# Three layer normalizations of layer 0 applied by ScalarE instead of VectorE

## The chip, the core and the metric

The kernel runs on one core of a Trainium2 chip, as a single launch. A core has five engines that run side by side, each with its own queue of instructions: TensorE (PE in the profile, with its weight loads as PEld), VectorE (DVE), ScalarE (ACT), GpSimd (POOL) and SyncE (SP), which here only issues DMAs. An engine takes its instructions in the order in which the program lists them; it waits at an instruction until the semaphores that this instruction names are reached. The metric is the time on the device in microseconds (us), lower is better.

## The reference, cut to what matters

Two layers over 4 sequences of 1024 tokens with 256 features, all fp32. Each layer computes `x = x + s * silu(...)` from a normalized `xn`:

```python
xn = _layernorm(x)                       # no gain, no bias
s = _L0_attn_ref(xn, ...)                # attention over cos/sin features, then an MLP
g = _silu(_L0_ffn_ref(xn, ...))          # token-shift FFN
x = x + s * g
xn = _layernorm(x)
s = _L1_attn_ref(xn, ...)                # selective scan (16 states, 512 channels)
g = _silu(_L1_ffn_ref(xn, ...))          # 8 experts, 2 per token, each with a norm
x = x + s * g
```

Inside `_L0_attn_ref` two more norms stand, both with gain and bias: `x2 = LN(x)` ahead of the queries, keys and values, and `x2 = LN(x + attention)` ahead of the MLP. Applying a norm to a token is `(x - mean) * rstd`, which is also `rstd * x + (-mean * rstd)`: a scale and a shift for each token.

## The kernel before

Layer 0 works on blocks of 512 tokens (`TB`), eight in all, two for each sequence. A block is a tile of 128 partitions with 4 x 256 numbers: a partition holds four tokens (`NT` = 4), and so a norm is applied with four instructions of 128x256, each with its own mean and rstd per partition. `normalize` (L499 to L518) gets them: bn_stats and bn_aggr on VectorE, the variance plus eps, then a power of -1/2 on GpSimd (L509). `apply` (L520) does `(x - mean) * rstd` on VectorE; all its instructions carry line L522.

There are four applies for each block:

- The attention norm (tile `x`, statistics `mv_a`, `rs2_a`), in `before_attention`. Two norms are folded into one here.
- The token norm (tile `x`, statistics `mv_a`, `rs_a`, kept from the attention norm), at the start of `after_attention`, on a block that is fetched anew. PE transposes its result (`tr_xnb`), and ACT copies that to `xnt`.
- The x3 norm (tile `x3_b` from `x`, statistics `mv_b`, `rs_b`), after the attention output is added. Right behind it VectorE adds a bias to the same `x` (L617). PE transposes x3 (`tr_b`), ACT writes `x3t`, and the MLP follows.
- The gate norm (tile `x`, statistics `mv_cb`, `rs_cb`), at the end of the block. Its result goes to HBM (`xn_d`), through PE (`tr_gb`) and ACT (`xg_b`) to the expert gate (`pgt_b`, added to `gate` at L715) and to the scan's input `xt_d`.

The attention itself runs in 64 groups of features (`cycle`): PE projects (`fk`, `fq`), ACT rounds (L764), VectorE takes the fraction (L765) and its magnitude (L397), ACT takes two sines, PE accumulates (`kv`, `pa`). The sines and the exponentials of the scan are in different tables of ACT, which is why there are 134 table loads (L488).

The scan of layer 1 runs beside layer 0 as soon as the first block is ready. A step of a unit (16 steps to a unit, 16 units) is: ACT takes two exponentials (the decays `da`, up to three steps ahead), VectorE multiplies (L1014), scans (L1017 or L1023) and multiplies again (L1032), and PE transposes and sums the result in PSUM (`y`). The steps between (L914 to L932) prepare a unit. When the last gate is there, VectorE computes the routes, GpSimd scatters the tokens to slots, and the experts' tiles run beside the rest of the scans (`es`, L1334, is the first thing that VectorE does with an expert's output). Their norm, too, is applied on ACT, with scale and shift (L1389 and L1391).

The order on each engine isn't that of the code. `arrange` (at the end of the kernel) takes all instructions with their dependences, plays them through with costs of its own, and writes an order for PE, VectorE and ACT by hand as scheduling dependences. Among the instructions that are ready on an engine, the one with the lowest due time goes first; the due time is the place in the code plus an entry of the table `LATER`, by engine and by the name of the tile written (for ACT in layer 0: `x` 47, `xi` 189, `da` 415). What it assumes for an instruction's cost:

```python
if engine == "Activation":
    w = 165 + 0.84 * n + 75 * min(scalars, 1)
...
    w = 160 + (1.053 if psum else 0.516) * n + 60 * scalars      # tensor_scalar on DVE
```

The small statistics and shifts come from the pool `small`, two buffers to a tag.

Of the kernel before, what the change touches and what calls it, by code (L numbers as in the profile page):

```python
# [15 lines left out]
F32 = mybir.dt.float32  # L16
U32 = mybir.dt.uint32
AF = mybir.ActivationFunctionType
ALU = mybir.AluOpType
# [4 lines left out]
P = 128  # L24
# [3 lines left out]
NT = TB // P  # L28
# [336 lines left out]
def kernel(  # L365
# [3 lines left out]
    nc = tc.nc  # L369
# [19 lines left out]
    def col(name, i=0):  # L389
        return vec[:, COL[name] + i : COL[name] + i + 1]  # L390

    def tokens(ap):
        return ap.rearrange("(t p) d -> p t d", p=P)
# [15 lines left out]
    small = ctx.enter_context(tc.tile_pool(name="small", bufs=2))  # L409
# [13 lines left out]
    def fetch_x(j):  # L423
        t = work.tile([P, NT, D], F32, name=f"x_{j}_{nc.next_id()}", tag="w")
        nc.gpsimd.dma_start(out=t, in_=tokens(x[j * TB : (j + 1) * TB, :]))
        return t
# [71 lines left out]
    def normalize(pool, src, tag, twice=False):  # L498


        st = small.tile([P, NT, 6], F32, name=f"st_{tag}", tag="ln_st")
        bufs = 4 if twice else 2
        mv = pool.tile([P, NT, 2], F32, name=f"mv_{tag}", tag="ln_mv", bufs=bufs)
        rs = pool.tile([P, NT], F32, name=f"rs_{tag}", tag="ln_rs", bufs=bufs)
        for t in range(NT):
            nc.vector.bn_stats(st[:, t, :], src[:, t, :])  # L506
            nc.vector.bn_aggr(mv[:, t, :], st[:, t, :])
        nc.vector.tensor_scalar(rs, mv[:, :, 1], EPS, None, ALU.add)
        nc.gpsimd.tensor_tensor(rs, rs, mhalf, ALU.pow)  # L509
        if not twice:  # L510
            return mv, rs
        both = small.tile([P, NT], F32, name=f"rs2_{tag}", tag="ln_rs2")
        nc.vector.tensor_tensor(both, rs, rs, ALU.mult)
        nc.vector.tensor_tensor(both, both, mv[:, :, 1], ALU.mult)
        nc.vector.tensor_scalar(both, both, EPS, None, ALU.add)
        nc.gpsimd.tensor_tensor(both, both, mhalf, ALU.pow)
        nc.vector.tensor_tensor(both, both, rs, ALU.mult)
        return mv, rs, both  # L518

    def apply(dst, src, mv, rs):  # L520
        for t in range(NT):
            nc.vector.tensor_scalar(  # L522
                dst[:, t, :], src[:, t, :], mv[:, t, 0:1], rs[:, t : t + 1], ALU.subtract, ALU.mult
            )
# [9 lines left out]
    keys, kept = {}, {}  # L534

    def bias(n, tiles=NT):

        return bias_s[:, n : n + 1, :].to_broadcast([P, tiles, D])

    def before_attention(b, s):  # L540
# [5 lines left out]
        mv, rs, both = normalize(keep, xi, tag, twice=True)  # L546
        kept[j] = (mv, rs)
        apply(xi, xi, mv, both)
        yield "N"
        x2t = work.tile([P, NC, TB], F32, name=f"x2t_{tag}", tag="w")  # L550
# [31 lines left out]
    def after_attention(b, s, at):  # L582

        j = b * (L // TB) + s
        tag = f"b{j}"
        x1 = fetch_x(j)
        yield "N"
        apply(x1, x1, *kept.pop(j))
        yield "N"
        xnt = keep.tile([P, NC, TB + 1], F32, name=f"xnt_{tag}", tag="xnt")  # L590
        if s == 0:
# [21 lines left out]
        yield "N"  # L613
        mv, rs = normalize(small, x1, tag)
        x3 = work.tile([P, NT, D], F32, name=f"x3_{tag}", tag="w")
        apply(x3, x1, mv, rs)
        nc.vector.tensor_tensor(x1, x1, bias(2), ALU.add)  # L617
        yield "N"
        x3t = work.tile([P, NC, TB], F32, name=f"x3t_{tag}", tag="w")
        for c in range(NC):  # L620
            nc.scalar.activation(
                x3t[:, c, :], transposed(x3, c, f"{tag}{c}"), AF.Identity,
                bias=col("ln2_b", c), scale=col("ln2_g", c),
# [72 lines left out]
        xi = fetch_x(j)  # L696
# [2 lines left out]
        nc.vector.tensor_tensor(x1, x1, xi, ALU.add)  # L699
        nc.gpsimd.dma_start(out=tokens(x_mid[j]), in_=x1)  # L700
        mv, rs = normalize(small, x1, f"c{tag}")
        apply(xi, x1, mv, rs)
        nc.gpsimd.dma_start(out=tokens(xn_d[j]), in_=xi)
        yield "N"
        xt = work.tile([P, NC, TB], F32, name=f"xg_{tag}", tag="w")
# [824 lines left out]
    for b in range(NB):  # L1530
        groups = [("k", b, s, t) for s in range(2) for t in range(NT)]
        groups += [("q", b, s, m, par) for s in range(2) for m in range(NC) for par in range(2)]
        for c, group in enumerate(groups):
            if c == 0:
                before.add(before_attention(b, 1))
            elif c == 4:
                while before.force():
                    pass
            elif c == 12 and b + 1 < NB:
                before.add(before_attention(b + 1, 0))  # L1540
            if before.wants == "K" and c >= 12:
                before.wants = "N"
            cycle(group, quota=(2, 3 if scans.ahead else 6, 2 if scans.ahead else 6, 0))
            for s in range(2):
                if len(at.get((b, s), ())) == NC:
                    after.add(after_attention(b, s, at.pop((b, s))))
            if 0 in ready and not blocks and not scans.side.todo:
                scans.side.add(first_unit())
                while not units:
                    scans.side.force()  # L1550
        while before.force():
            pass
# [87 lines left out]
```

## Time and profile before

| | us |
|---|---|
| median of 3 runs | 2220.71 |
| lowest and highest | 2216.21, 2221.44 |
| the profiled execution, its own run | 2219.3 |
| its span, first to last instruction | 2217.6 |
| PE busy | 1776.2 (80%) |
| DVE busy | 1939.0 (87%) |
| ACT busy | 1389.7 (63%) |
| POOL busy | 501.2 (23%) |
| mean granted TensorE clock | 0.88 |

The profile is of one execution. A slice line gives an engine's busy share in 40 equal slices of the span, in tenths. A group's row reads: line, engine, operation, out<-in, shapes and count; then after the first bar the busy time of all of them together and the mean length of one in ns (neighbours overlap a little, so busy time divided by the count is less than the mean); after the second bar the time that the engine stood idle just before them, and what ended it. In the timeline each row is the start, the length and the instruction, and in square brackets the idle time before it with what released it. A row of the window view gives the length, then busy us and instruction counts of PE, PEld, DVE, ACT and POOL, then the granted clock, the share of the DMA engines, and GB/s.

### The profile page before, as it was taken

The page shows a single profiled execution, that of the slowest core. Times are in us where ns is not written, and L with a number is a line of the kernel's source. Part 1 is how long each engine was busy: PE and PEld are TensorE (multiplying, and loading weights), DVE is VectorE, ACT ScalarE, POOL GpSimd, SP SyncE. Part 2 cuts the span into 40 slices and gives each one's busy share as a digit, 9 for nine tenths or more (in the row PEclk, how much of TensorE's full clock was granted, in tenths as well). Part 3 has the DMA queues.
Part 4 walks back from the last instruction along what each step waited for, and adds up shares of the span by engine and source line. Part 5 has one row for each costly group of instructions (what it writes and reads, how often), then busy time and mean ns, then how long its engine had stood idle before and what let it go on. Part 6 is the DMA issues. An engine that isn't in the chain of part 4 may idle for free. (4 is left out here: it accounts for less than half of the span.)

```text
span 2217.6 us, 25392 instructions
## 1 busy us (share of the span) xinstructions
PE 1776.2 (80%) x9192; PEld 1232.7 (56%) x9192; DVE 1939.0 (87%) x2508; ACT 1389.7 (63%) x2039; POOL 501.2 (23%) x459
## 2 busy tenths in 40 slices
PE   6789679789987889969888777367988879899754
PEld 3335346444654545645456555256777658778643
DVE  4582669999999899889999999858998999989998
ACT  4664468797887788697875264334554555455584
POOL 1000100101100111000010110844544435445210
PEclk9789789789998989979998796588999989999877
DMA  9601123323332332323334354666777857877553
GB/s 274 170 19 48 57 87 103 107 68 95 83 108 85 115 86 78 105 75 107 114 89 136 117 159 128 164 200 202 227 243 222 240 200 247 280 230 224 190 191 103
DMA packets 145086, 320.22 MB, mean 144 GB/s; under 512 B 23344, under 2 KB 43952, under 8 KB 139072
## 3 DMA queue, kind: packets, MB, share of 16 engines
q1 hardware_dynamic: 110704, 170.02, 28.8%
q0 software_dynamic: 34256, 148.58, 19.3%
q8 instruction: 73, 1.20, 0.2%
q14 instruction: 53, 0.43, 0.1%
HBM read 256.86 MB, written 61.69 MB: 144 GB/s over the span
## 5 line engine op out<-in xcount | busy, mean ns | idle before, releaser
L496 ACT ACTIVATE da<-dt,neg_a 128x512 f32<-128x512 f32 x512 | 336.0, 715 | 157.1 <-PE y L1035 101.1
L1035 PE MATMUL y<-ident,da 128*128 128x128 f32 x2048 | 304.6, 298 | 126.8 <-DVE da L1032 120.3
L1035 PEld LDWEIGHTS y<-ident,da 128*128 128x128 f32 x2048 | 257.8, 154 | 193.3 <-DVE da L1032 95.8
L1032 DVE TENSOR_TENSOR da<-h,bcs 128x1024 f32<-128x1024 f32 x256 | 311.2, 1217 | 0.9
L1017 DVE TENSOR_TENSOR_SCAN h<-da,h 128x1024 f32<-128x1024 f32 x128 | 290.9, 2281 | 10.7 <-ACT da L496 8.8
L1014 DVE TENSOR_TENSOR h<-dtu,bcs 128x1024 f32<-128x1024 f32 x240 | 287.8, 1212 | 9.9 <-DMA bcs<-bcd 9.3
L1023 DVE TENSOR_TENSOR_SCAN h<-da,h_tail,h 128x512 f32<-128x512 f32 x224 | 277.2, 1268 | 8.8 <-ACT da L496 8.0
L403 PE MATMUL ph<-xst,we 128*128 128x256 f32 x736 | 178.9, 396 | 10.0 <-ACT xst L1309 9.3
L488 ACT ACT_TABLE_LOAD x134 | 171.9, 1283 | 3.2 <-PEq L1625 0.8
L403 PE MATMUL po<-we,ht 128*128 128x256 f32 x736 | 171.0, 385 | 1.1 <-ACT ht L1321 0.9
L403 PEld LDWEIGHTS ph<-xst,we 128*128 128x128 f32 x736 | 141.7, 198 | 34.6 <-ACT xst L1309 12.9
L403 PEld LDWEIGHTS po<-we,ht 128*128 128x128 f32 x736 | 139.6, 193 | 31.0 <-issue 6.6
L403 PE MATMUL ph_b<-x3t_b,w_b 128*128 128x512 f32 x256 | 119.8, 618 | 9.6 <-DVE fs_k L765 5.2
L403 PE MATMUL py_b<-w_b,ht_b 128*128 128x256 f32 x512 | 116.8, 385 | 4.7 <-ACT ht_b L643 1.7
L1321 ACT ACTIVATE ht<-ph,we 128x256 f32<-128x256 f32 x184 | 76.7, 470 | 65.0 <-PE ph L403 52.2
L403 PEld LDWEIGHTS py_b<-w_b,ht_b 128*128 128x128 f32 x512 | 97.4, 193 | 23.2 <-ACT ht_b L643 3.4
L801 PE MATMUL kv<-fs_k,v_a 128*32 128x256 f32 x1024 | 84.2, 475 | 29.6 <-ACT fs_k L496 29.6
L1309 ACT COPY xst<-pxs 128x512 f32<-128x512 f32 x46 | 26.9, 585 | 120.6 <-PE pxs L1305 120.6
L1272 POOL DMA_INDIRECT fused<-xs x46 | 86.4, 1878 | 44.5 <-DVE xs L1338 32.0
L1272 POOL DMA_INDIRECT slots<-xs x46 | 89.8, 1953 | 18.5 <-issue 10.1
L765 DVE SCALAR_TENSOR_TENSOR fs_k<-fs_k,fk 128x512 f32<-128x512 f32 x128 | 80.0, 678 | 15.7 <-ACT fs_k L764 15.7
L832 PE MATMUL pa<-fs_q,kvp 128*32 128x512 f32 x512 | 83.5, 675 | 12.5 <-ACT fs_q L496 12.5
(239 smaller groups left out, 3388.9 us busy)
## 6 DMA issues: line engine op xcount, KB each, us to landing
bcs<-bcd SPq DMA_DIRECT2D x240, 512.0 KB, 5.2
xs<-slots POOLq DMA_DIRECT2D x23, 516.0 KB, 4.9
x<-in_x_dram POOLq DMA_DIRECT2D x23, 512.0 KB, 5.2
slots<-blank SPq DMA_DIRECT2D x1, 11776.0 KB, 48.9
w_b<-in_w_dram POOLq DMA_DIRECT2D x16, 512.0 KB, 4.4
w_b<-in_w_dram POOLq DMA_DIRECT2D x32, 256.0 KB, 3.0
xs<-slots POOLq DMA_DIRECT2D x23, 260.0 KB, 3.9
slots<-blank SPq DMA_DIRECT2D x1, 5888.0 KB, 26.2
```

The source lines that it names most:

```text
L403: nc.tensor.matmul(ps, lhs, rhs, start=i == 0, stop=i == len(pairs) - 1)
L488: nc.scalar.preload_act_table_set({"E": "natural_log_exp_and_others", "S": "silu_and_others"}[which])
L496: in_turn(nc.scalar.activation(out, in_, func, **kw))
L765: nc.vector.scalar_tensor_tensor(t[:, 1, :], t[:, 0, :], -ROUND, ps[r], ALU.add, ALU.subtract)
L801: nc.tensor.matmul(kv[b][r // 2][32 * g : 32 * g + 32, r % 2, :, :], v[:, t, h * DH : (h + 2) * DH], f[:, :, m, par, :], start=(s, t, r % ...
L832: nc.tensor.matmul(pa[b, s][32 * r : 32 * r + 32, :], kvp[b][:, e, 4 * m + r, par, :], features(fs, r)[:, e, :], start=(par, e) == (0, 0), ...
L1014: nc.vector.tensor_tensor(h, dtu, bcs[:, 0:1, :].to_broadcast([P, UNIT, TB]), ALU.mult)
L1017: nc.vector.tensor_tensor_scan(flat, da.rearrange("p w t -> p (w t)"), flat, 0.0, ALU.mult, ALU.add)
L1023: nc.vector.tensor_tensor_scan(h[:, w, :], da[:, w, :], b[w], h_tail[:, c, n : n + 1], ALU.mult, ALU.add,)
L1032: nc.vector.tensor_tensor(da, h, bcs[:, 1:2, :].to_broadcast([P, UNIT, TB]), ALU.mult)
L1035: nc.tensor.matmul(y[:, t, w * P : (w + 1) * P], da[:, w, t * P : (t + 1) * P], ident, is_transpose=True, start=False, stop=(n, t % 2, w) ...
L1272: i = nc.gpsimd.indirect_dma_start(out=dst, out_offset=IndirectOffsetOnAxis(ap=index, axis=0), in_=src, in_offset=None)
```

## The change

A new helper, `apply_by_scalar`, computes the shift `-mean * rstd` for the four tokens of each partition with one small instruction on VectorE (128x4), and then applies scale and shift with four activations (Identity) on ScalarE. The token norm, the x3 norm and the gate norm use it; the attention norm stays on VectorE.

```diff
+    def apply_by_scalar(dst, src, mv, rs, tag):
+        shift = small.tile([P, NT], F32, name=f"shift_{tag}", tag="ln_shift")
+        nc.vector.scalar_tensor_tensor(shift, mv[:, :, 0], -1.0, rs, ALU.mult, ALU.mult)
+        for t in range(NT):
+            nc.scalar.activation(
+                dst[:, t, :], src[:, t, :], AF.Identity, bias=shift[:, t : t + 1],
+                scale=rs[:, t : t + 1],
+            )
+
     def apply(dst, src, mv, rs):
         for t in range(NT):
             nc.vector.tensor_scalar(
...
         x1 = fetch_x(j)
         yield "N"
-        apply(x1, x1, *kept.pop(j))
+        apply_by_scalar(x1, x1, *kept.pop(j), f"k{tag}")
...
         x3 = work.tile([P, NT, D], F32, name=f"x3_{tag}", tag="w")
-        apply(x3, x1, mv, rs)
+        apply_by_scalar(x3, x1, mv, rs, f"b{tag}")
         nc.vector.tensor_tensor(x1, x1, bias(2), ALU.add)
...
         mv, rs = normalize(small, x1, f"c{tag}")
-        apply(xi, x1, mv, rs)
+        apply_by_scalar(xi, x1, mv, rs, f"c{tag}")
         nc.gpsimd.dma_start(out=tokens(xn_d[j]), in_=xi)
```

`arrange` then makes its order anew from the changed list. In the program that it gives, ACT has 96 activations more and VectorE 72 instructions fewer (96 applies gone, 24 shifts added); all others are the same in number, the table loads among them. They keep their order nearly everywhere: in layer 0 an instruction of VectorE is moved past 2 others on the mean and at most 34; from the routing on, nothing is moved.

## The prediction

> **What bounds the kernel now.** I read the slices of the page first, then busy time by stage, then the waits of the engine that is full, and last the stretches around the places that the change touches.
>
> ```profile
> DVE  4582669999999899889999999858998999989998
> ACT  4664468797887788697875264334554555455584
> ```
>
> ```profile
> 0.00:330.00 330.00, 249.50 (x1244) 134.01 (x1244) 184.29 (x365) 177.52 (x261) 32.93 (x59) 0.84 0.40 109
> 330.00:1100.00 770.00, 654.16 (x3632) 404.05 (x3632) 721.02 (x978) 631.29 (x827) 80.65 (x98) 0.91 0.33 94
> 1100.00:1340.00 240.00, 192.90 (x869) 136.31 (x866) 232.46 (x275) 136.17 (x191) 32.91 (x48) 0.85 0.45 133
> ```
>
> The columns of the second view are the length, busy us of PE, PEld, DVE, ACT and POOL, the granted clock, and DMA. Layer 0 ends near 1340 us. In its first 330 us nobody is full (DVE 56%): there the chain of projections and features sets the pace. From 330 to 1100, scans of layer 1 run beside layer 0, and DVE is busy 721 of 770 us (94%) with ACT at 631 (82%). From 1100 to 1340 DVE is at 97%, ACT at 57%.
>
> After 1340 nothing changes: in the built program all five engines have the same order from there on. The end hangs on layer 0 through the routing: DVE works gaplessly to the slots (1387 us), GpSimd scatters 32 times, and DVE stands until the first expert tile comes out:
>
> ```profile
> 1472.14 0.69 DVE L1334 TENSOR_TENSOR es<-po,we 128x512 f32<-128x512 f32 x1 [20.62 <-PE po L403]
> ```
>
> So what DVE gains or loses before 1387 us reaches the end one for one, and the question is its busy time plus its idle time there.
>
> **The change, part by part.** The durations:
>
> ```profile
> L522 DVE TENSOR_SCALAR x<-x,mv_a,rs_a 128x256 f32<-128x256 f32 x60 | 21.7, 419 | 0.1
> ...
> L522 DVE TENSOR_SCALAR x<-x,mv_cb,rs_cb 128x256 f32<-128x256 f32 x32 | 11.4, 418 | 1.2 <-POOL rs_cb L509 1.1
> L522 DVE TENSOR_SCALAR x_b<-x,mv_b,rs_b 128x256 f32<-128x256 f32 x32 | 11.4, 414 | 3.2 <-POOL rs_b L509 2.9
> ...
> L1389 DVE SCALAR_TENSOR_TENSOR shift_d<-mv_d,rs_d 128x4 f32<-128x4 f32 x8 | 1.2, 146 | 0.0
> ```
>
> ```profile
> L1391 ACT ACTIVATE rows<-rows,shift_d,rs_d 128x256 f32<-128x256 f32 x32 | 16.6, 589 | 12.9 <-DVE shift_d L1389 12.8
> ```
>
> Removed from DVE: 32 applies of the x3 norm (11.4 us), 32 of the gate norm (11.4), and the 32 of the first row that are the token norm (21.7 x 32/60 = 11.6): 34.4 us. Added to DVE: 24 shifts at 0.15 us, 3.6. Net 30.8 us, 1.28 for each of 24 groups of four. Added to ACT: 96 activations with two pointers; L1391 is the same instruction in the same size, 16.6/32 = 0.52 us each: 49.8 us, 2.07 a group. Table loads stay at 134, since Identity needs no switch.
>
> A rule of the Trainium skill speaks against it: "ScalarE: Activation LUTs", section "Rules for kernel authors", gives add and mul to VectorE, because ScalarE is slower at them. The rows agree on the price (0.52 against 0.36 us). If the two engines stood in one chain, the price alone would count: 49.8 + 3.6 - 34.4 = 19 us slower. By occupancy it is DVE that is full, and 30.8 us come off. Neither holds everywhere, so I go place by place. The ACT place of each group is taken from the built program's order, its surroundings from 20 us of the trace behind it.
>
> *First 330 us* (all three groups of block 0, two of block 1): DVE is not full, so its 1.28 us buy nothing. Where the apply waits for the power on GpSimd and transposes wait for the apply (x3 of blocks 0 and 1, the gate norm of block 0), the chain was four on DVE (1.38 us) and becomes a shift and four on ACT (0.15 + 2.07): +0.8 each, +2.4 us.
>
> *Loose places* (nine groups: token and x3 norm of block 2; x3 norm of 4 and 5; gate norm of 1 and 6; all three of 7). ACT has idle behind them, DVE has none:
>
> ```profile
> 1105.00:1125.00 20.00, 12.48 (x61) 6.85 (x62) 20.00 (x28) 19.33 (x25) 0.36 (x1) 0.83 0.19 33
> ...
> 1231.00:1251.00 20.00, 10.95 (x44) 9.54 (x45) 17.71 (x31) 4.05 (x7) 1.86 (x1) 0.67 0.25 70
> ```
>
> In the second line ACT (fourth busy column) is busy 4 of 20 us: there 2.07 us vanish. Full credit is 9 x 1.28 = 11.5 us. But DVE and ACT run in lockstep in the features: L765 on DVE begins within 0.4 us of the end of its rounding L764 on ACT in half of the 179 cases between 330 and 1340 us, and where ACT is not itself held by DVE, a DVE that comes early just waits. Ends: 0 and -11.5. I take 60%, nearer the full credit, since most of these stretches show ACT waiting: -6.9.
>
> *Tight places* (ten groups in five pairs: gate norm of block 2 with the token norm of 3; x3 and gate norm of 3, with the token norm of 4; gate norm of 4 with token norm of 5; of 5 with 6; x3 of 6). The first line above is one: DVE 20.0 and ACT 19.3 of 20. I followed the pair at 952 us, where both are near 20 from 952 to 987:
>
> ```profile
> 965.34 2.43 ACT L764 ACTIVATE fs_k<-fk,round_c 128x512 f32<-128x512 f32 x4 [0.60 <-PE kv L801]
> ```
>
> ```profile
> 955.59 2.28 DVE L1017 TENSOR_TENSOR_SCAN h<-da,h 128x1024 f32<-128x1024 f32 x1
> 957.79 1.19 DVE L914 TENSOR_TENSOR dt<-dt,ln 128x1024 f32<-128x1024 f32 x1
> ...
> 966.43 0.68 DVE L765 SCALAR_TENSOR_TENSOR fs_k<-fs_k,fk 128x512 f32<-128x512 f32 x1
> ...
> 979.81 2.48 DVE L765 SCALAR_TENSOR_TENSOR fs_k<-fs_k,fk 128x512 f32<-128x512 f32 x4 [0.93 <-ACT fs_k L764]
> ```
>
> Four applies enter ACT's queue at 952.4, ahead of the decays (da) and the logarithm that DVE's scan and L914 need. DVE, 1.2 us early, waits for the decay until 955.1. The new order pulls the next scan (2.28 us) forward; its decay is behind the gate copies, which wait for the transposes of what ACT just wrote, so another 0.8 us: L914 starts at 960.5, where 957.79 + 2.28 = 960.1 would be no change. ACT is 3.2 us late now, 2.6 after its 0.60 idle. DVE loses the token norm's apply (-1.3) and has 2.4 us more scan work in front of L765: it gets there at 968.0, the rounding ends at 968.6. Then four more applies: ACT is 4.7 late, the next rounding ends at 984.5; DVE comes with 4.4 us of pulled work at 983.3 and starts at 984.5, against 979.81 + 4.4 = 984.2. The pair ends 0.3 to 0.9 us late instead of 2.56 early: +0.6. Five pairs: +3.0. Ends: ACT fully the bound, 10 x 2.07 = +20.7; or more scans pulled forward and the credit kept, -12.8. The worked pair stands nearer the middle.
>
> *What else moves.* L617 (x1 plus the last bias, 8 times) now waits until ACT has read x1; it stood right behind the apply on DVE, and in the new order scans stand before it (two in block 3): hidden behind those 2.5 us, else 2 us each with the whole DVE queue behind. The stores of xn and the fetches behind them on GpSimd's queue wait for ACT instead of DVE: 2 us later, with POOL busy 81 of 770 us, nothing; SP's queue keeps its order but for shifts of one or two places. PE's transposes come some 1.5 us later with matmuls queued behind them; PE is busy 654 of 770 us, and this is in the pairs already. The last gate norm stands on ACT behind a silu and a table load, some 6 us later than now; the new order puts about 7 us of scans ahead of the gate add on DVE, which covers it. Last, the planner's table of due times has no entry for the shifts, and its entry for x on ACT now delays the applies too: bounds 0 and +10; I take +2.
>
> Sum: +2.4 - 6.9 + 3.0 + 2 = +0.5 us on the profiled execution (span 2217.6, run 2219.3, 1.4 below the median of the runs). On the median 2220.7 that is 2221.
>
> **The rivals.**
> *A, the forecast (0.44):* the stalls take the gain back: -9 to +10 about +0.5.
> *B, ACT becomes the bound in the tight pairs (0.32):* decays and roundings stand behind the applies, DVE runs out of scans whose decays are ready, and each tight group costs its full 2.07: +2.4 - 6.9 + 20.7 = +16, 2237. It decides where ACT's lateness exceeds the scan work in front of the next L765, 2.4 and 4.4 us in the worked pair. For it: ACT at 19.3 to 19.9 of 20 us there. Against it: DVE waits only 13.4 us on decays in L1023 and L1017 from 330 to 1340, so scans have some room.
> *C, DVE's relief goes through (0.24):* -11.5 in the loose places, half to all of -12.8 in the tight: with +2.4, -15 to -22; I put it at -14 with some lockstep, 2207. For it: DVE 94 to 97% full, ACT 82 and 57%. Against it: the handoff within 0.4 us.
> That the change does not do what it says is excluded: the built program has 96 applies more on ACT and 72 instructions fewer on DVE.
>
> **How the numbers follow.** A measurement of this kernel tells a difference from none at about 0.3%, 6.7 us. A gives 0.28 within, 0.05 faster, 0.11 slower; B 0.29 slower, 0.03 within; C 0.23 faster, 0.01 within. Together 0.28 faster, 0.32 same, 0.40 slower. The range reaches to 2204 (a little past C's point) and 2240 (past B's), which leaves one in ten on either side. A's own range is 2212 to 2231.
>
> **What would show it.** DVE busy falls by about 31 us and ACT's rises by about 50 in total. Right: DVE's waits on ACT (da, fs_k, ln) between 330 and 1340 us grow by about 20 us over the roughly 30 there now, and the first expert sum, at 1472 now, moves by less than 5 us. B: they grow by 35 or more, and it comes near 1488. C: they grow by less than 12, and it comes near 1458. I am wrong altogether if the change of the time arises after that point, where the order is the same, or if the loss sits in waits for PE or in the granted clock.

## The result, and the profile after

The changed kernel takes 2247.13 us (median of 4 runs, 2244.44 to 2248.37) where the kernel before takes 2221.07 (4 runs, 2216.21 to 2223.11): the ratio is 1.0111, 95% interval 1.0092 to 1.0131. It is 26 us slower; the forecast was 2221 with a range up to 2240. The profiled execution took 2248.3 us, its span is 2246.6, its granted clock 0.877 (before 0.88).

The two slice lines and the three stages of the page after, to be laid beside those of before:

```profile
DVE  4572569898989897989789899799899999989998
ACT  3673568797888797797785545324554455455584
```

```profile
0.00:330.00 330.00, 247.14 (x1212) 131.45 (x1216) 175.06 (x347) 184.71 (x275) 32.91 (x59) 0.83 0.40 106
330.00:1100.00 770.00, 645.77 (x3559) 394.80 (x3560) 680.66 (x898) 631.01 (x844) 75.86 (x93) 0.91 0.32 93
1100.00:1340.00 240.00, 194.31 (x865) 132.34 (x864) 222.17 (x259) 149.97 (x219) 24.67 (x28) 0.86 0.37 109
```

The granted clock of the middle row is 0.91, as before. ScalarE did as much in it as before, 631.0 us against 631.3, although it now also has applies to do. The view of line L524 alone, in the same stretch (ACT busy us, count):

```profile
330.00:1100.00 770.00, 25.20 (x48) 0.91 0.32 93
```

So of its old work ScalarE had done 631.0 - 25.2 = 605.8 us by 1100, 25.5 us less than before. VectorE is behind as well. It was busy 680.7 us where before it had 721.0, but little of that is relief. The applies that stand on it before (line L522), then after (L531, the attention norm alone) and the shifts (L522 after), in the same stretch:

```profile
330.00:1100.00 770.00, 24.53 (x68) 0.91 0.33 94
```

```profile
330.00:1100.00 770.00, 5.72 (x16) 0.91 0.32 93
330.00:1100.00 770.00, 1.74 (x12) 0.91 0.32 93
```

24.53 - 5.72 - 1.74 = 17 us have gone from it; the other 23 are work that it had not reached by 1100. All of layer 0 is late by some such amount, and these rows alone don't say which engine is the cause. The first expert sum, which stood at 1472.14, comes 31 us later:

```profile
1503.33 0.66 DVE L1343 TENSOR_TENSOR es<-po,we 128x512 f32<-128x512 f32 x1
```

The applies themselves are as priced. Groups of the page's form, the shift of the normalization that was on ScalarE all along last:

```profile
L524 ACT ACTIVATE x<-x,shift_cb,rs_cb 128x256 f32<-128x256 f32 x32 | 16.9, 592 | 11.4 <-DVE shift_cb L522 11.4
L524 ACT ACTIVATE x_b<-x,shift_bb,rs_b 128x256 f32<-128x256 f32 x32 | 16.8, 591 | 10.7 <-DVE shift_bb L522 10.7
L524 ACT ACTIVATE x<-x,shift_kb,rs_a 128x256 f32<-128x256 f32 x32 | 16.7, 592 | 10.8 <-DMA x<-in_x_dram 8.6 <-issue 2.1
L1400 ACT ACTIVATE rows<-rows,shift_d,rs_d 128x256 f32<-128x256 f32 x32 | 16.6, 589 | 13.8 <-DVE shift_d L1398 13.7
...
L539 PE MATMUL tr_gb<-ident,x 128*128 128x128 f32 x64 | 16.1, 398 | 34.1 <-ACT x L524 34.0
```

50.4 us in all, 0.52 us each. ScalarE stands 33 us at the heads of these groups until a shift or a fetched x arrives, with everything behind it in its queue standing too, and PE's transposes of the gate norm wait 34 us for the applies.

Where each kernel runs late against before, in us, at the same instruction (the times of before in the head: starts of five roundings of features on ScalarE, ends of the last gate add, of the routing, of the first expert sum and of the last row):

| | 397 | 594 | 786 | 832 | 1104 | gate 1336 | routing 1387 | expert 1473 | last 2210 |
|---|---|---|---|---|---|---|---|---|---|
| after | +3.7 | +7.6 | +16.5 | +23.5 | +36.9 | +40.4 | +35.1 | +31.2 | +28.9 |
| dve_new_order | +6.6 | +6.9 | +17.9 | +25.1 | +37.4 | +46.0 | +41.0 | +35.8 | +32.7 |
| act_old_order | +9.8 | +13.4 | +25.9 | +32.4 | +43.1 | +64.7 | +60.6 | +57.2 | +60.8 |
| replan_100 | +4.0 | -0.2 | +6.4 | +10.9 | +15.0 | +21.8 | +28.8 | +27.2 | +39.3 |
| tight_only | -0.2 | -1.0 | +9.0 | +14.8 | +23.5 | +18.8 | +19.5 | +19.6 | +26.6 |
| loose_only | +0.2 | +4.6 | +4.9 | +5.9 | +6.7 | +16.3 | +11.0 | +5.2 | +3.0 |
| after_refit2 | +2.2 | -3.6 | +1.5 | +0.3 | +4.9 | +18.5 | +13.0 | +15.1 | +31.7 |
| after_refit3 | +2.1 | -3.5 | +1.6 | -1.0 | +4.8 | +19.1 | +14.3 | +18.6 | +19.2 |
| tight_refit | +2.6 | -1.2 | +7.2 | +2.8 | +16.3 | +14.6 | +14.3 | +17.0 | +16.3 |
| loose_refit | -5.0 | -4.1 | -2.6 | -5.6 | -2.0 | +3.7 | -0.2 | -3.2 | -13.7 |
| before_refit2 | +0.5 | -8.4 | -9.2 | -12.5 | -9.7 | -7.2 | -11.6 | -9.8 | -3.4 |

The loss grows through layer 0, is complete at the last gate, and 9 us of it are given back before the first expert sum. (These are single executions; verdicts below rest on the ratios.)

VectorE's waits between 330 and 1340 us, before first, then after (what waited for what: us in total, times, longest):

```profile
DVE h L1023 <- ACT da L496: 8.0, 3, 4.4
...
DVE h L1017 <- ACT da L496: 5.4, 3, 4.0
...
DVE h L1014 <- DMA bcs<-bcd: 1.9, 4, 0.9
```

```profile
DVE h L1032 <- ACT da L496: 14.9, 5, 6.9
DVE h L1023 <- DMA bcs<-bcd: 12.7, 11, 2.7
DVE h L1026 <- ACT da L496: 9.5, 7, 2.7
...
DVE u L885 <- ACT u L881: 5.9, 5, 2.5
...
DVE dt L923 <- ACT ln L496: 4.4, 1, 4.4
```

All its waits on ScalarE rise from 30.4 to 57.2 us in that stretch, those on PE from 19.0 to 27.2, and the scans' wait for their broadcast rows (bcs, a DMA) from 1.9 to 12.7: the scans are reached before their inputs are there. In *dve_new_order* (below), where VectorE has no relief, they rise nearly as far: to 46.8 on ScalarE and 10.9 for bcs.

One stretch shows it at the scale of single instructions. ScalarE from the rounding of one feature group to the next (fs_q<-fq), first before, then after:

```profile
786.00 2.41 ACT L764 ACTIVATE fs_q<-fq,round_c 128x512 f32<-128x512 f32 x4
...
789.04 1.28 ACT L488 ACT_TABLE_LOAD   x1
...
798.17 1.28 ACT L488 ACT_TABLE_LOAD   x1
...
804.12 2.43 ACT L764 ACTIVATE fs_q<-fq,round_c 128x512 f32<-128x512 f32 x4
```

```profile
802.45 2.42 ACT L773 ACTIVATE fs_q<-fq,round_c 128x512 f32<-128x512 f32 x4 [0.60 <-PE fq L749]
...
805.50 1.28 ACT L488 ACT_TABLE_LOAD   x1
...
808.13 0.58 ACT L850 COPY at<-pa 128x512 f32<-128x512 f32 x1
...
813.87 1.28 ACT L488 ACT_TABLE_LOAD   x1
815.16 2.07 ACT L524 ACTIVATE x<-x,shift_kb,rs_a 128x256 f32<-128x256 f32 x4
...
821.89 1.28 ACT L488 ACT_TABLE_LOAD   x1
823.19 0.58 ACT L850 COPY at<-pa 128x512 f32<-128x512 f32 x1
...
824.90 1.86 ACT L773 ACTIVATE fs_q<-fq,round_c 128x512 f32<-128x512 f32 x3
```

Between the two roundings ScalarE has no idle time in either kernel. Before, the stretch is 18.12 us; after, 22.45. The difference of 4.33 has two parts: 2.07 are the four applies, and about 2.4 are work that the new order has put in front of the rounding, one more table load (1.28) and two copies (2 x 0.58). The number of table loads in the whole kernel is unchanged (134); it is only where they stand. So in this one stretch the cost is half applies and half order. In dve_new_order, which has nearly the new order but no applies on ScalarE, the same stretch is 2.6 us longer than before for another reason: it has one table load where before has two, but ScalarE stands 4.8 us in it waiting for PE and VectorE.

### The profile page after: what moved, and what is told of

It reads as the page before. It is cut to its first block, busy times and chain, and to the rows that moved or that the text cites. A ratio compares the mean times of both kernels' runs of the same rounds, so it can differ in the third digit from the quotient of the medians.

```text
span 2246.6 us, 25439 instructions
## 1 busy us (share of the span) xinstructions
PE 1788.6 (80%) x9192; PEld 1234.0 (55%) x9192; DVE 1909.7 (85%) x2436; ACT 1435.1 (64%) x2135; POOL 481.7 (21%) x459
## 5 line engine op out<-in xcount | busy, mean ns | idle before, releaser
L1023 DVE TENSOR_TENSOR h<-dtu,bcs 128x1024 f32<-128x1024 f32 x240 | 288.7, 1212 | 23.9 <-DMA bcs<-bcd 23.5
L403 PE MATMUL ph_b<-x3t_b,w_b 128*128 128x512 f32 x256 | 125.9, 644 | 14.6 <-DVE fs_q L774 7.4
L403 PEld LDWEIGHTS ph_b<-x3t_b,w_b 128*128 128x128 f32 x256 | 51.2, 206 | 76.7 <-issue 51.0
```

The source lines that it names most:

```text
L403: nc.tensor.matmul(ps, lhs, rhs, start=i == 0, stop=i == len(pairs) - 1)
L1023: nc.vector.tensor_tensor(h, dtu, bcs[:, 0:1, :].to_broadcast([P, UNIT, TB]), ALU.mult)
```

## The experiments

The comparison is always with the kernel before on the same chip. "Table" is `LATER`, the planner's table of offsets; "the planner's clock" is the end time that `arrange` itself arrives at.

### Engine and order apart

*dve_new_order*: the kernel before, whose planner takes the applies of the three norms for ScalarE's (the cut lines pick them). Its order is almost that of after (an instruction of VectorE 0.30 places away on the mean, of PE 0.56), but the applies are still VectorE's and there are no shifts.

```diff
+        own = x.engine
...
+            x.engine, x.weight, x.hidden = 'Activation', 455.0, 90.0
+        x.own = own
...
-                order.setdefault(engine, []).extend(x.all)
+                order.setdefault(x.own, []).extend(x.all)
```

> The kernel before, with all applies on VectorE, but the planner is told that the three kinds of apply run on ScalarE (455 ns each), so that PE, VectorE, ScalarE and GpSimd get nearly the order of the changed kernel. If the loss comes from the order (theory Order), about 2240 to 2250 us, as the changed kernel. If it comes from ScalarE's time on the feature chain (theory ScalarE), about 2215 to 2228, near the kernel before. Half and half: 2235.

Measured 2252.78 us, 1.0138 (1.0111 to 1.0166). No work has changed engine, and the loss is that of after; so is the curve of lateness in the table. Its middle stage:

```profile
330.00:1100.00 770.00, 647.70 (x3571) 402.42 (x3573) 696.85 (x937) 610.39 (x797) 77.65 (x94) 0.89 0.32 93
```

ScalarE, without a single apply, has done 20.9 us less by 1100 than the 631.29 of before. So most of the 25.5 us that it is behind in after can come from the order alone. But the order is one for other engines than the work has here, so this run doesn't measure what the order costs in after.

*act_old_order*: the reverse, after's code with the planner told that the applies are VectorE's at 412 ns and that the shifts cost nothing, so that the order stays near that of before (1.34 places on VectorE, 2.29 on PE).

```diff
+        own = x.engine
...
+            x.engine, x.weight, x.hidden = 'DVE', 412.0, 90.0
+        x.own = own
...
+            x.weight, x.hidden = 0.0, 0.0
```

> The changed kernel, but the planner is told that the applies run on VectorE (412 ns each) and that the shifts cost nothing, so that the order stays near that of the kernel before, with the applies where VectorE had them. Theory Order: near the kernel before, 2215 to 2228 us. Theory ScalarE: at least the changed kernel's 2247, up to 2265, since nothing is planned around the longer ScalarE queue.

Measured 2280.74 us, 1.0257 (1.0227 to 1.0287): the worst of all. Each order fits the engines it was planned for better than the others. The new order is not a mistake of the planner; given the move, it saves some 32 us (1.0257 against 1.0111) over one near the old.

*replan_100* and *replan_c*: the kernel before with its planner disturbed in another way, nothing changed in the work.

```diff
-SIGNAL, LANDING, PER_BYTE = 60.0, 2000.0, 1 / 260
+SIGNAL, LANDING, PER_BYTE = 100.0, 2000.0, 1 / 260
```

> The kernel before, all applies on VectorE; only the planner's assumed cost of a semaphore is 100 ns instead of 60. Its order then differs from that of the kernel before about as much as the changed kernel's does (VectorE's instructions are moved by 2.4 places on the mean in both). If any new plan of this size loses what was gained by fitting the due times to the old one (theory Replan): +15 to +30 us. If the loss is of ScalarE's applies: within 7 us of the kernel before.

```diff
+        own = x.engine
...
+            x.weight = 80.0
```

(The line stands under a condition that picks the applies of the three norms.)

> The kernel before, all applies on VectorE, planned as if the three kinds of apply took 80 ns each instead of 412: an order that is meant for a relieved VectorE and is moved by 1.6 places on the mean. Theory Replan: +10 to +25 us. Theory ScalarE: within 7 us.

replan_100: 2259.39 us, 1.0145 (1.0110 to 1.0179), with instructions of VectorE moved 2.44 places on the mean and of PE 3.90; the move of after is 2.39 and 3.82. replan_c: 2227.55 us, 1.0015 (1.0000 to 1.0030), with 1.60 and 2.56 places. A new order of the size that after has can cost as much as the whole result, and need not.

### By place and by kind

*loose_only* and *tight_only*: the nine and the ten groups of the prediction on ScalarE, the rest on VectorE as before.

```diff
+    def by_scalar(kind, j):      # loose_only
+        return (kind, j) in {("c", 1), ("k", 2), ("b", 2), ("b", 4), ("b", 5), ("c", 6), ("k", 7), ("b", 7), ("c", 7)}
+                                 # tight_only
+        return (kind, j) in {("c", 2), ("k", 3), ("b", 3), ("c", 3), ("k", 4), ("c", 4), ("k", 5), ("c", 5), ("k", 6), ("b", 6)}
...
-        apply_by_scalar(x3, x1, mv, rs, f"b{tag}")
+        if by_scalar("b", j):
+            apply_by_scalar(x3, x1, mv, rs, f"b{tag}")
+        else:
+            apply(x3, x1, mv, rs)
```

> ScalarE applies only the nine groups that the prediction called loose; the rest stays on VectorE. The prediction's steps: -6.9 us, so about 2214; at most -11.5. If ScalarE's 2.07 us per group reach the end wherever they stand: 9 x 2.07 = up to +18, about 2235. If the loss sits in the tight places alone: 2210 to 2221.

> ScalarE applies only the ten groups that the prediction called tight. The prediction's steps: +3, about 2224. Its rival B, where ScalarE is the bound there: +21, about 2242. If the loss is spread over all groups alike (26 us over 24): +11, about 2232.

loose_only: 2222.52 us, 0.9999 (0.9981 to 1.0016). tight_only: 2241.24 us, 1.0080 (1.0051 to 1.0109), 18 us. The tight places carry most of the loss.

The traces show where on the way it comes about. Nine of the ten tight groups lie in four stretches between two roundings (starts in before: 633.65 to 701.18, 769.27 to 832.71, 949.99 to 1018.78, 1086.63 to 1117.46); the x3 norm of block 6 comes behind them, and of the loose groups those of x3 of blocks 4 and 5 lie in them too. What each stretch adds to the lateness, in us, with the lateness at 1117 behind it:

| | 634-701 | 769-833 | 950-1019 | 1087-1117 | sum | late at 1117 |
|---|---|---|---|---|---|---|
| after | +7.3 | +9.5 | +6.2 | +6.5 | +29.5 | +36.2 |
| tight_only | +7.9 | +8.0 | +3.4 | +6.6 | +25.9 | +23.1 |
| loose_only | +1.0 | +1.9 | +1.2 | +0.2 | +4.3 | +6.6 |
| dve_new_order | +7.6 | +11.7 | +7.4 | +6.8 | +33.6 | +39.4 |
| replan_100 | +4.1 | +6.5 | +4.2 | +2.9 | +17.8 | +14.0 |

Most of after's loss arises in these four stretches, as rival B of the prediction had it. But dve_new_order and replan_100, with every apply on VectorE, lose in the same four: what is dear there is a new order, with or without more work for ScalarE.

The second of them and the loose stretch behind it, between the same roundings, in before, after and dve_new_order:

```profile
769.27:832.71 63.44, 50.43 (x227) 27.67 (x226) 61.17 (x107) 52.87 (x75) 10.58 (x13) 0.88 0.29 83
832.71:949.99 117.28, 109.58 (x643) 69.32 (x640) 101.89 (x132) 91.10 (x122) 14.31 (x17) 0.98 0.32 90
```

```profile
783.25:856.16 72.91, 56.22 (x251) 30.04 (x250) 67.42 (x107) 58.82 (x86) 11.75 (x13) 0.86 0.23 73
856.16:970.95 114.79, 105.06 (x618) 66.23 (x618) 92.61 (x124) 91.44 (x122) 12.44 (x17) 0.99 0.30 92
```

```profile
782.61:857.79 75.18, 56.49 (x248) 32.47 (x248) 69.26 (x114) 53.27 (x75) 11.01 (x13) 0.84 0.23 70
857.79:972.17 114.38, 104.69 (x617) 66.23 (x617) 92.55 (x124) 91.58 (x122) 12.45 (x17) 0.99 0.32 92
```

The new order pulls scans forward into the tight stretch: at its end VectorE has done 96 scan instructions in after and in dve_new_order, 92 in before. It is 9.5 and 11.7 us longer. In the stretch behind it they are missing, and at its end all three kernels have done 106. But with 9.3 us less work for VectorE that stretch is only 2.5 us shorter (2.9 in dve_new_order): PE is busy 93% of it before and VectorE 87%, and it isn't VectorE's work that sets its length. What is pulled forward costs time in one place and is not paid back in the other.

*token_only*, *gate_only*, *x3_only*: one of the three norms on ScalarE, in all eight blocks (`by_scalar` returns `kind == "k"`, `"c"`, `"b"`).

> ScalarE applies the token norm alone, 8 groups, four of them in tight pairs. If ScalarE's time is the price (2.07 us in each of the four tight ones, nothing elsewhere): +8, about 2230. If the wait of PE's transposes for the apply is the price: near 0, since this norm has the least to wait for. By the prediction's steps: +1.

> ScalarE applies the gate norm alone, 8 groups, four of them in tight pairs. ScalarE's time: +8, about 2230. If the longer chain from the statistics over the power and the shift to the transposes is the price, more here than for the token norm: +12 or more. By the prediction's steps: +1.

> Only the second normalization (x3, 8 x 4 applies) is on ScalarE, the token's and the gate's stay on VectorE. Theory 1 (what counts is how the old table orders the new assignment; planner's clock 2181.4 against 2170.2 for before, and measured differences have been about 0.75 of that clock's): slower by 8 us, 2230 (2224 to 2236). Theory 2 (each apply has a cost of its own, and the costs add: token alone +24, gate alone +10, all three +26): the x3 would come out 8 us faster than before, 2213; with a third of the loss each, 2230.

1.0080 (1.0048 to 1.0112), 1.0035 (1.0022 to 1.0048) and 1.0066 (1.0042 to 1.0089). They add to 1.8%, and all three together cost 1.1%: each kernel has an order of its own, and the prices do not add.

### A table fitted anew

The table has an offset for most names, and was made when the applies were VectorE's. With it the planner's own clock ends at 2170.2 us for the kernel before and at 2204.2 for after; it had the 26 us in it (34 by its count). I searched new offsets by random steps, keeping those that the planner's clock did not dislike, and did the same for the kernel before as a control.

```diff
-            "da": 16, "dt": 119, "kvp": -38, "ln": 144, "mu_k": 27, "mv_c": -59, "rs": -185,
-            "rs_c": -554, "st_c": -270, "u": 70
...
+    'DVE': {'da': 16, 'dt': -75, 'ln': 157, 'mv_c': -398, 'rs': -59, 'rs_c': -1715, 'st_c': -94, 'u': 11,
...
+    'shift_b': -35, 'shift_k': -793,
...
+    'shift_c': -761,
...
```

> The changed kernel with nothing altered but the planner's table of offsets (LATER). New offsets were looked for on the planner's own clock, which says 2204.2 us for the changed kernel with the old table, 2170.2 for the kernel before with the old table, and 2172.2 for the changed kernel with this one. Theory 1 (the loss is that of a table fitted to the old assignment of engines): most of the 26 us comes back, 2222 us (2212 to 2232), and the lag of the last layer-0 gate against before falls from 40 us to under 15. Theory 2 (ScalarE is simply the slower engine for this work, or its in-order waits at the applies cost it whatever the order): the time stays at 2240 to 2250.

> The kernel before, its table of offsets searched anew in the same way and for as long (planner's clock 2170.2 -> 2164.4 us). It is the control for after_refit: how much a fresh search gives where nothing has changed engine. Theory 1: little, since the old table was fitted to this assignment: 2217 us (2210 to 2224). If the search gives 20 us here as well, then after_refit shows only that the search is good, not that the table was misfitted by the change.

after_refit (the best of three searches, clock 2172.2): 2236.89 us, 1.0061 (1.0037 to 1.0086). before_refit (one search, clock 2164.4): 2217.22 us, 0.9982 (0.9967 to 0.9997). Of 25 us, 11 are gone; the control gains 4. Neither theory had this: part of the loss is the table's, and part stays.

*after_refit2*: the search carried on (clock 2169.7), the table alone changed. *after_refit3*: its first half kept, its second (from the routing on) put back to the old one. *dve_refit_order2*: after_refit2's table in dve_new_order, so that VectorE applies in an order planned for ScalarE (0.70 places on VectorE and 1.19 on PE from that of after_refit2).

> The changed kernel again with only its table of offsets searched further (planner's clock 2204.2 with the old table, 2172.2 in after_refit, 2169.7 here). Theory 1 (what is left of the loss is plan as well): a little faster than after_refit, 2233 us (2226 to 2238). Theory 2 (about 13 us are ScalarE's own and no table takes them away): the same as after_refit, 2236 (2232 to 2241).

> after_refit2 with the second half of its table (from the routing on, where no apply changes engine) put back to the old one; the first half stays the searched one. after_refit2 had layer 0 back to 0.7 us behind before at 1087 us and the routing 13 us behind, but lost 17 us more behind the routing. Theory 1 (that later loss came from the searched second half of the table, and the changed layer 0 itself owes only what is left at the routing): the routing again about 13 us late, and the end no later than that, 2234 us (2228 to 2240). Theory 2 (the MoE part is late because of what layer 0 left behind, scans not done in time): the loss stays, 2250 (2244 to 2256).

> The order of after_refit2 as nearly as the planner gives it (the kernel before, whose planner is told that the three kinds of apply run on ScalarE at 455 ns, with the table of after_refit2), but the applies run on VectorE as before and no shifts are computed. It puts a price on the engine alone in an order fitted to ScalarE. Theory 1 (in a fitted order the move gains, as it did in the unfitted one, where VectorE was 6 us slower than ScalarE): slower than after_refit2 by 5 to 12 us, 2243 (2236 to 2250). Theory 2 (the 13 us left in after_refit are ScalarE's price): faster than after_refit2 by about 13 us, 2222 (2216 to 2228).

after_refit2: 2252.07 us, 1.0120 (1.0097 to 1.0143), outside both expectations: a better planner's clock, a worse time. The table of lateness says where: at 1104 us it is 4.9 late, where after was 36.9, at the routing 13.0, and then it loses 17 more in the experts, whose part of the table had been searched too. after_refit3: 2235.70 us, 1.0045 (1.0026 to 1.0064): the second half of the table was the culprit. Its middle stage, whole and with the applies alone:

```profile
330.00:1100.00 770.00, 647.60 (x3682) 397.66 (x3681) 709.17 (x943) 659.34 (x886) 86.77 (x98) 0.92 0.33 95
```

```profile
330.00:1100.00 770.00, 27.17 (x52) 0.92 0.33 95
```

659.3 - 27.2 = 632.2 us of ScalarE's old work are done by 1100, as many as before (631.3), with four more applies besides than in after: up to there the refitted order has made up for the move, measured against the kernel before with its old table. Against before_refit2 (the kernel before with a searched table, below) it is 14.5 us late at 1104. Between 1104 and the last gate come another 14 us, of which the routing gives back 5.

dve_refit_order2: 2273.66 us, 1.0214 (1.0190 to 1.0239). In an order planned for ScalarE, VectorE is the worse engine for the applies by 0.9% (1.0214/1.0120, as near as the two orders are). That is against the second theory, but as in dve_new_order the order was planned for the other engine; what ScalarE's share is in the 13 us left in after_refit, it doesn't say.

*loose_refit*, *before_refit2*, *tight_refit*: the nine loose groups, the kernel before, and the ten tight groups, each with a searched table. loose_refit and tight_refit start from that of before_refit and reach clocks of 2165.0 and 2173.6; before_refit2 goes on from before_refit (2162.6). The searches were not of equal length, and that of tight_refit was the shortest.

> The nine loose groups of applies on ScalarE (loose_only, which was level with before at 0.9999), with a table searched anew from that of before_refit (planner's clock 2185.8 with the old table, 2165.0 here, against 2164.4 for before_refit and 2170.2 for before). Theory 1 (VectorE's relief is worth nothing where the order is fitted, since the chain of layer 0 and not VectorE's sum sets the routing): level with before_refit, 2217 us (2211 to 2223). Theory 2 (relief in loose places goes through, 7 us by the prediction's own sum, and was hidden in loose_only by the misfit of the table): 2210 (2205 to 2214), which would beat both kernels.

> The kernel before with a table searched as long as that of loose_refit and longer (planner's clock 2162.6; before_refit 2164.4, loose_refit 2165.0). Control for loose_refit, which ran at 0.9932. Theory 1 (what loose_refit gained is a lucky table, VectorE's relief has no part in it): level with loose_refit, 2210 us (2204 to 2214). Theory 2 (relief in the loose places goes through once the table fits): level with before_refit, 2218 us (2214 to 2224).

> The ten tight groups on ScalarE (tight_only, 1.008 with the old table) with a table searched anew from that of before_refit, about as many steps as loose_refit had (planner's clock 2185.6 with the old table, 2173.6 here; loose_refit 2165.0, before_refit2 2162.6). Theory 1 (what is left of the loss with a fitted table is the tight places, where ScalarE has no idle time): above before, 2233 us (2226 to 2240), where the nine loose groups ran at 2211. Theory 2 (place does not matter once the table fits; after_refit3 was only less well searched): level with loose_refit and before_refit2, 2212 (2206 to 2218).

| | median us | ratio to before | interval |
|---|---|---|---|
| loose_refit | 2211.49 | 0.9932 | 0.9914 to 0.9951 |
| before_refit2 | 2213.39 | 0.9960 | 0.9937 to 0.9983 |
| after_refit3 | 2235.70 | 1.0045 | 1.0026 to 1.0064 |
| tight_refit | 2241.83 | 1.0063 | 1.0036 to 1.0090 |

With fitted tables loose and tight still stand 1.3% apart, intervals clear of each other: the tight places did not pay with either table. But each row is one order that a search came upon, and orders of the same work lie as far apart (1.0145 and 1.0015 above), so how much of the 1.3% is the place and how much the search isn't shown. Fitted against fitted, the whole change costs 0.85% (1.0045/0.9960), some 19 us of the 25. loose_refit beats both kernels, before by 0.68% and after by 1.8% (0.9932/1.0111). Against before_refit2 its interval overlaps, so whether VectorE's relief has a part in that, or the searched table has it all, stays open.

## Why the prediction was wrong

*What bounds the kernel* held in its frame: what layer 0 loses reaches the end, and behind the routing the order is the same. Not quite one for one: of 35.1 us at the routing 28.9 are left in the last row. The sum that the prediction named, VectorE's busy time plus its idle time up to the slots, in before, after and dve_new_order:

```profile
0.00:1387.10 1387.10, 1129.91 (x5884) 698.67 (x5884) 1183.16 (x1678) 963.30 (x1305) 147.91 (x213) 0.88 0.37 104
```

```profile
0.00:1422.20 1422.20, 1142.95 (x5892) 699.74 (x5892) 1158.80 (x1609) 1011.02 (x1404) 148.35 (x213) 0.87 0.36 102
```

```profile
0.00:1428.10 1428.10, 1149.63 (x5892) 709.93 (x5892) 1188.47 (x1682) 965.92 (x1308) 150.43 (x213) 0.86 0.36 102
```

After against before: busy -24 us, idle 203.9 to 263.4, +59. The relief came; the idle time is what the forecast had too small. dve_new_order has +36 of it without any relief.

*The prices* held. VectorE's busy time fell from 1939.0 to 1909.7 us (29.3; forecast 30.8), ScalarE's rose from 1389.7 to 1435.1 (45.4; forecast 49.8), an activation is 0.52 us.

*First 330 us, +2.4*: the lateness at 397 us is 3.7. A little small.

*Loose places, -6.9*: loose_only is level, 0 with an interval of -4 to +4 us. The credit did not come; the end of its range without credit (0) was right. A table fitted to them lets them be faster than before, but so does one fitted to before.

*Tight places, +3.0*: the step that failed. tight_only is 18 us slower, tight_refit 14; the bound "ACT fully the bound" had been +20.7. In the pair that I followed and carried over to all five, the rounding was to end 4.7 us late, and 4.4 of these were taken off because VectorE would do that much scan work ahead. The roundings ahead of the pair and at its end, before and then after:

```profile
949.99 2.41 ACT L764 ACTIVATE fs_k<-fk,round_c 128x512 f32<-128x512 f32 x4
...
979.11 2.40 ACT L764 ACTIVATE fs_k<-fk,round_c 128x512 f32<-128x512 f32 x4
```

```profile
970.95 2.40 ACT L773 ACTIVATE fs_k<-fk,round_c 128x512 f32<-128x512 f32 x4
...
1002.90 2.42 ACT L773 ACTIVATE fs_k<-fk,round_c 128x512 f32<-128x512 f32 x4
```

They are 20.96 and 23.79 us late, so the pair delays the rounding by 2.8, less than forecast. What failed is the credit: nothing is paid back. At 1086.63 the scans are level with before (122 done in both), and the rounding there is 29.8 late. The stretch from 769 to 950 us shows it more plainly: four scans pulled forward, 9.5 us lost, 2.5 regained. Scans done ahead of time would be worth their full time only where VectorE sets the length of what follows. Its 94% over the stage is an average; from 832 to 950 it is PE that is busy 93%.

How much of the tight places' loss is ScalarE's own time (at most 10 x 2.07 = 20.7 us, by the prediction's sum) and how much the new order there, the runs do not separate: dve_new_order loses as much in the same stretches with no apply on ScalarE.

*The planner's table of due times, +2 (0 to +10)*: too small as well, by how much is open. I had looked for entries that meet the new instructions, and took the order as unchanged because an instruction moved past 2 others on the mean. dve_new_order puts that order, with no work moved, at +1.4%, some 31 us; replan_100 puts a different one of the same size at the same, replan_c one at +0.15%. That a new order of this size can cost 30 us or next to nothing was not in my sum at all. The two steps are no separate terms either: dve_new_order's loss, the engine's in the old order (act_old_order, 57 us) and after's 25 do not add. The misfit of the table itself looks smaller: fitting gives back 15 us (1.0111 to 1.0045), but the control gained 9, so 6 us are left for it, within my 0 to +10. With a fitted table the tight places alone still cost 14 us and the loose ones nothing. Why the last blocks, between 1104 us and the last gate, lose 14 us even in after_refit3 is not shown.

*L617 and the last gate norm*: L626 (as it is now) waited 4.6 us in all, small as said. The scans ahead of the last gate add did cover it: VectorE has no idle time in front of that add at 1376.46. They make it late themselves, 40.4 us, 3.5 more than the last rounding listed at 1104, and 5.3 of that are back at the routing (35.1).

*The rivals.* B, ScalarE as the bound in the tight pairs, was right in its place and nearest in its time (2237, where the measured 2247 lies beyond it); that ScalarE's time is the reason isn't shown. Its mark, VectorE's waits on ScalarE grown by 35 us, was not met: they grew by 26.8 (30.4 to 57.2), nearer to the 20 that I gave for the forecast, whose other mark, the first expert sum moved by less than 5 us, failed with 31. The rule of the Trainium skill that the prediction weighed ("ScalarE: Activation LUTs", "Rules for kernel authors": add and mul belong to VectorE) gave +19 for one chain. The time came out near it, but by luck: at 0.8 us a group (19/24) the nine loose groups would have cost 7 us and the ten tight ones 8, and they cost 0 and 18. The price per instruction is not what decided.

## What to carry to other kernels

In a kernel whose order is fitted to where each piece of work runs, moving work to another engine is two changes: the move, and a new order that nobody has fitted. Measure them apart (the new order with the old engines, and the reverse), and fit the order again before you judge the move, with the kernel before fitted as long beside it. To see where time is lost, compare the two kernels between the same two instructions, stretch by stretch, and not over a fixed time, in which every engine of a late kernel has done less. An engine that is 94% busy over a whole stage can still have stretches in which another one sets the pace, and work that is taken from it or done ahead buys little there.

## What the runs showed that was not expected

- The order alone is worth more than the change. With the same work, an order whose VectorE instructions are 2.4 places from before's on the mean ran at 1.0145 (replan_100), one that is 1.6 away at 1.0015 (replan_c), one that is 0.66 away at 0.9960 (before_refit2): 1.85% between them. The size of the displacement doesn't decide: in the traces loose_refit, the fastest of all, is about 2 places away on the mean.
- The planner's clock had the sign and about the size of the change (34 us for 26), but tells nothing at a few us: 2169.7 (after_refit2) ran at 1.0120 and 2172.2 (after_refit) at 1.0061.
- ScalarE's 33 us at the heads of the apply groups, no more than 9 of them for fetches of x, are not waits on top of those it had: between 330 and 1340 us its waits for VectorE fell from 48.6 to 38.1 in after. PE's waits for ScalarE rose there from 25.9 to 63.9.
